# First layer of a two-layer kernel: the spreading of B goes ahead of the sum in TensorE's queue

## The chip, the core and the metric

The kernel runs on one core of one Trainium2 chip. The metric is the device time of one execution in microseconds. Before the change it is 6610.32 us, the median of three runs between 6605.85 and 6630.87 us; the profiled execution spans 6600.6 us.

## What is computed

Two layers follow one another on an input of 4 images of 48 x 48 points with 128 channels. Only the first is touched here. It is a selective scan (a state-space layer) over each image in four directions. Cut to what matters:

```python
xz = einsum(gn(x), in_proj_w); xin, z = split(xz)          # 256 inner channels
xc = silu(depthwise 3x3 convolution of xin)
xs = [xc rows first, xc columns first, and both reversed]    # K = 4 directions, L = 2304 points
dts_r, Bs, Cs = split(einsum(xs, x_proj_w))                 # R = 8, N = 16 states each
dt = softplus(einsum(dts_r, dt_proj_w) + dt_proj_b)
for l in range(L):                                           # for every channel d and state n
    h = h * exp(dt[l] * A) + (dt[l] * xs[l]) * B[l, n]
    y[l] = sum over n of h * C[l, n]
y = y + Ds * xs;  sum of the four directions;  layer norm;  * silu(z);  out_proj;  + x
```

B and C are the same for all channels, and differ by state and by point. The second layer (a Fourier neural operator with attention) starts when the first has ended.

## The kernel before

The channels lie on the partitions, in NF = 2 halves of 128. A direction is cut into chunks of 480 points (the last has 384), and a chunk into N = 16 steps, one for each state. There are 4 x 4 x 5 x 16 = 1280 steps. The work of a step is spread over the engines:

```python
def fetch(u):       # SP: C of two states, broadcast to all partitions by DMA (and B of every fourth state)
def drive_pool(u):  # POOL, for i % 4 == 3 alone: db = du * bbc
    u.db = three.tile([128, NF, LC], F32, tag="db", ...)
    if i % 4 == POOLS: nc.gpsimd.tensor_mul(u.db, c.du, u.bbc)                     # line 329
def spread(u):      # PE, for the other three: B of the state on all 128 partitions, by a matmul
    if i == N - 1: done[0] = c.number + 1
    if i % 4 == POOLS: return
    u.pb = ps_b.tile([128, 512], F32, tag="pb", ...)                                # one buffer
    nc.tensor.matmul(u.pb[:, 0:n], pick[:, i:i+1].to_broadcast([NX, 128]), c.bs[:, 0:n])   # line 339
def drive_in(u):    # DVE, for those three: db = du * pb
    if i % 4 != POOLS: nc.vector.tensor_mul(u.db, c.du, u.pb)                       # line 346
def decay(u):       # ACT: da = exp(dt * A), into PSUM, for each half
    for f in range(NF): nc.scalar.activation(da, c.dt[:, f], AF.Exp, scale=a_neg)   # line 356
def scan(u):        # DVE: h = da * h_before + db along the chunk, for each half
    u.h = three.tile([128, NF, LC], F32, tag="h", ...)                              # three buffers
    for f in range(NF): nc.vector.tensor_tensor_scan(...)                           # line 367
def read_out(u):    # POOL: hc = h * C
    u.hc = three.tile([128, NF, LC], F32, tag="hc", ...)                            # three buffers
    nc.gpsimd.tensor_mul(u.hc, u.h, u.cbc)                                          # line 372
def carry_on(u):    # ACT: the last h, for the next chunk                            # line 375
def sum_up(u):      # PE: adds hc of the 16 states in PSUM, by matmuls with the identity
    if i == 0: ...  # starts the sum with Ds * xc, or with y of the directions before   # lines 384, 389
    for f in range(NF):
        nc.tensor.matmul(c.yp[f], ident, u.hc[:, f], start=False, stop=(i == N - 1))   # line 391
    ...             # after the last state ACT copies yp out                        # lines 399, 406
```

The PSUM pools of the layer are ps_s (2 buffers, for the pieces below), ps_b (1, for pb), ps_a (3, for da) and ps_y (2, for the two halves of yp).

Each call of `advance` starts one step and issues one stage of each of the steps under way. The number is the lag in steps; the order in the tuple is the order of issue, and so the order in each engine's queue. At its end comes one piece of background work: the projections of the next direction's chunks (`project`: px, pd, bs, dt), the front of the next image (`front`: normalization, input projection pj, convolution pc), or the end of a past one (`back`).

```python
LAGS = (
    (0, fetch), (3, drive_pool), (4, drive_in), (5, scan), (4, decay), (5, read_out), (6, carry_on),
    (7, sum_up), (3, spread),
)
def advance(u):
    window.appendleft(u)
    for lag, stage in LAGS:
        if window[lag] is not None:
            stage(window[lag])
    piece()
```

In the middle of each chunk (i = 8) `drive` has POOL compute du = dt * xc of the chunk to come, in two halves (line 245). `project` has POOL compute two small differences for each chunk (lines 227 and 233), which make bs carry B in three bf16 parts.

Of the kernel before, what the change touches and what calls it, by code (L numbers as in the profile page):

```python
# [35 lines left out]
def layer0(ctx, tc, io, x1_dram):  # L36
# [391 lines left out]
    def drain(gen):  # L428
# [3 lines left out]

    LAGS = (
        (0, fetch), (3, drive_pool), (4, drive_in), (5, scan), (4, decay), (5, read_out), (6, carry_on),
        (7, sum_up), (3, spread),
    )
    window = deque([None] * 8, 8)

# [683 lines left out]
```

## Time and profile before

| | before |
|---|---|
| time, median of 3 | 6610.32 us |
| span of the profiled execution | 6600.6 us |
| DVE (VectorE) busy | 5361.8 us, 81% |
| PE (TensorE) busy | 4939.4 us, 75% |
| POOL (GpSimd) busy | 4911.8 us, 74% |
| ACT (ScalarE) busy | 3055.7 us, 46% |
| granted TensorE clock, mean | 0.831 |
| first to last scan of the first layer | 132 to 4494 us |

Busy shares are averages over both layers; the first layer's loop is read by itself from the table of windows. In the list of waits, "A <- B" is idle time of A's engine that ended when B's instruction was done. In the timeline, each row is an instruction or several of one kind in sequence, with its start and its duration, and the idle time before it in brackets. A float32 matmul of the sum appears as two records, so that the two halves of a step make four.

### The profile page before, as it was taken

What the parts mean: (1) busy time and instruction counts of PE and PEld (TensorE: products, weight loads), DVE (VectorE), ACT (ScalarE), POOL (GpSimd) and SP (SyncE); (2) the same over time, 40 slices, a digit from 0 to 9 for tenths busy, and PEclk for the clock granted to TensorE, in tenths of its full rate; (3) what the DMA queues carried; (4) which work ended last, traced back from release to release, by engine and by line L of the source; (5) the groups of instructions that cost most, each with busy time, mean ns of one, the idle gap of its engine ahead of it and who ended that gap; (6) DMA issues with size and microseconds to landing.
All of it is one profiled execution on the core that took longest, in us unless ns stands there. A gap on an engine that the chain in (4) does not pass through costs nothing. (4 is left out here: it accounts for less than half of the span.)

```text
span 6600.6 us, 45820 instructions
## 1 busy us (share of the span) xinstructions
PE 4939.4 (75%) x12490; PEld 2183.8 (33%) x12490; DVE 5361.8 (81%) x5060; ACT 3055.7 (46%) x5657; POOL 4911.8 (74%) x2784
## 2 busy tenths in 40 slices
PE   7898778888887888987887778785323398878763
PEld 3343233334333334333333333332112244435332
DVE  1978889987888998888989888995699899963344
ACT  3656556655656665655666555553000133321222
POOL 2989889888988898898889989883466489951222
PEclk9899989999989999998999998997556655556876
DMA  1222222222223232222323322321300100010222
GB/s 39 89 88 90 93 88 95 88 92 87 91 93 90 89 98 87 92 92 87 96 87 101 91 93 91 93 87 47 68 0 0 16 7 4 4 39 8 58 58 57
DMA packets 271781, 457.67 MB, mean 69 GB/s; under 512 B 87134, under 2 KB 196734, under 8 KB 271522
## 3 DMA queue, kind: packets, MB, share of 16 engines
q1 hardware_dynamic: 224546, 438.13, 22.3%
q10 hardware_dynamic: 46976, 16.61, 1.4%
q8 instruction: 98, 1.61, 0.1%
q14 instruction: 161, 1.32, 0.1%
HBM read 419.60 MB, written 35.02 MB: 69 GB/s over the span
## 5 line engine op out<-in xcount | busy, mean ns | idle before, releaser
L372 POOL TENSOR_TENSOR hc<-h,cbc 128x960 f32<-128x960 f32 (+1 forms) x1280 | 2727.1, 2141 | 495.6 <-DVE h L367 292.5
L391 PE MATMUL yp<-hc,ident 128*128 128x480 f32 (+1 forms) x5120 | 2481.0, 610 | 672.1 <-POOL hc L372 666.7
L356 ACT ACTIVATE da<-dt,a_neg 128x480 f32<-128x480 f32 (+1 forms) x2560 | 1643.7, 647 | 1506.0 <-DVE h L367 1481.2
L367 DVE TENSOR_TENSOR_SCAN h<-da,carry,db 128x480 f32<-128x480 f32 (+1 forms) x2048 | 2304.0, 1175 | 41.6 <-ACT da L356 11.9
L391 PEld LDWEIGHTS yp<-hc,ident 128*128 128x128 f32 x5120 | 992.7, 204 | 2048.7 <-POOL hc L372 1196.8
L346 DVE TENSOR_TENSOR db<-du,pb 128x960 f32<-128x960 f32 (+1 forms) x960 | 1054.3, 1098 | 472.5 <-PE pb L339 423.9
L329 POOL TENSOR_TENSOR db<-du,bbc 128x960 f32<-128x960 f32 (+1 forms) x320 | 685.9, 2143 | 5.0 <-issue 2.5
L887 PE MATMUL py<-attn_t,xt 48*128 48x384 f32 x768 | 507.8, 846 | 78.7 <-DVE m L895 71.9
L367 DVE TENSOR_TENSOR_SCAN h<-da,db 128x384 f32<-128x384 f32 (+1 forms) x512 | 505.6, 1039 | 31.5 <-ACT da L356 24.3
L339 PE MATMUL pb<-bs,pick 112*128 112x480 bf16 (+1 forms) x960 | 368.7, 384 | 66.5 <-DVE db L346 64.0
L889 ACT COPY ysb<-py 128x384 f32<-128x384 f32 x384 | 184.0, 479 | 404.6 <-PE py L887 361.7
L887 PEld LDWEIGHTS py<-attn_t,xt 48*128 48x128 f32 x768 | 233.7, 320 | 339.9 <-issue 148.7
L176 PE MATMUL pc<-pad,cdiag 128*128 128x480 f32 (+1 forms) x720 | 294.0, 549 | 0.3 <-ACT pad L164 0.2
L375 ACT COPY carry<-h 128x2 f32<-128x2 f32 x1280 | 228.5, 179 | 3.7 <-DVE h L367 2.5
L807 PE MATMUL pat<-ident,s 48*48 48x48 f32 x128 | 13.3, 276 | 274.3 <-POOL s L803 274.3
L204 PE MATMUL px<-xc,w_xp 128*112 128x480 f32 (+1 forms) x320 | 212.9, 774 | 2.0 <-ACT xc L188 2.0
L245 POOL TENSOR_TENSOR du<-dt,xc 128x480 f32<-128x480 f32 (+1 forms) x160 | 202.0, 1283 | 7.7 <-DVE db L346 3.3
L900 POOL TENSOR_TENSOR zi<-zi,m 128x384 f32<-128x384 f32 x192 | 192.0, 1000 | 14.5
L898 POOL TENSOR_TENSOR zi<-gw,ysb 128x384 f32<-128x384 f32 x192 | 182.0, 948 | 25.7 <-ACT ysb L889 25.4
L899 POOL TENSOR_TENSOR m<-gw,ysb 128x384 f32<-128x384 f32 x192 | 185.4, 966 | 10.6 <-ACT ysb L889 10.6
L389 PE MATMUL yp<-y,ident 128*128 128x480 f32 (+1 forms) x240 | 170.6, 832 | 18.6 <-ACT y L406 18.3
L339 PEld LDWEIGHTS <-pick 112*128 112x128 bf16 x960 | 101.1, 105 | 251.5 <-issue 229.4
(263 smaller groups left out, 5808.2 us busy)
## 6 DMA issues: line engine op xcount, KB each, us to landing
cbc<-cd SPq DMA_DIRECT2D x512, 480.0 KB
bbc<-cd SPq DMA_DIRECT2D x256, 240.0 KB
cbc<-cd SPq DMA_DIRECT2D x128, 384.0 KB
bbc<-cd SPq DMA_DIRECT2D x64, 192.0 KB
da_wM<-a_wM SPq DMA_DIRECT2D x12, 396.0 KB
x<-in_xT SPq DMA_DIRECT2D x16, 288.0 KB
xr<-in_xT SPq DMA_DIRECT2D x16, 288.0 KB
e_wM<-de_wM SPq DMA_DIRECT2D x12, 384.0 KB
```

The source lines that it names most:

```text
L176: nc.tensor.matmul(pc[:, 0:n].rearrange("p (r c) -> p r c", c=H), cdiag[:, j], pad[:, r0 + dy : r0 + dy + nr, dx : dx + H], start=(j == 0) ...
L204: nc.tensor.matmul(like(px[0:NX, 0:n], k), w_xp[:, k, f], src[:, f], start=(f == 0), stop=(f == NF - 1))
L245: nc.gpsimd.tensor_mul(like(c.du[:, f, 0:n], c.k), like(c.dt[:, f, 0:n], c.k), src[:, f])
L329: nc.gpsimd.tensor_mul(u.db[:, :, 0:n], c.du[:, :, 0:n], u.bbc[:, :, 0:n].to_broadcast([128, NF, n]))
L339: nc.tensor.matmul(u.pb[:, 0:n], pick[:, i : i + 1].to_broadcast([NX, 128]), c.bs[:, 0:n], start=True, stop=True)
L346: nc.vector.tensor_mul(u.db[:, :, 0:n], c.du[:, :, 0:n], u.pb[:, None, 0:n].to_broadcast([128, NF, n]))
L356: nc.scalar.activation(da[:, 0:n], c.dt[:, f, 0:n], AF.Exp, scale=a_neg[:, q, i : i + 1])
L367: nc.vector.tensor_tensor_scan(ha, aa, ba, init, ALU.mult, ALU.add)
L372: nc.gpsimd.tensor_mul(u.hc[:, :, 0:n], u.h[:, :, 0:n], u.cbc.to_broadcast([128, NF, n]))
L375: nc.scalar.copy(carry[:, u.i], u.h[:, :, 0 if u.c.k >= 2 else u.c.n - 1])
L391: nc.tensor.matmul(c.yp[f][:, 0:n], ident, u.hc[:, f, 0:n], start=False, stop=(i == N - 1))
L887: nc.tensor.matmul(p[:, 0 : HG * T], xt[:, c, j], attn_t[:, b, hs], start=True, stop=True)
```

## The change

In the tuple that orders the stages, `spread` of step t-3 is moved ahead of `sum_up` of step t-7. Both are TensorE's alone, but for the copies of yp by ACT at the end of a chunk, so TensorE's queue has the two in the other order. Its purpose is that the spreading of B for a coming state need not stand in the queue behind a sum that waits for its product.

```diff
     LAGS = (
         (0, fetch), (3, drive_pool), (4, drive_in), (5, scan), (4, decay), (5, read_out), (6, carry_on),
-        (7, sum_up), (3, spread),
+        (3, spread), (7, sum_up),
     )
```

## The prediction

> **What bounds the kernel now.** I first read the page's row of slices, to see which part of the span the change can touch. Each digit is a tenth of busy time in a fortieth (165 us) of the span.
>
> ```profile
> PE   7898778888887888987887778785323398878763
> DVE  1978889987888998888989888995699899963344
> POOL 2989889888988898898889989883466489951222
> ```
>
> The first layer's scan loop fills slices 1 to 27: the scans of line 367 run from 132 to 4494 us, 4363 us of the 6601 us span. In it DVE and POOL are both at eight or nine tenths, and neither is full. The table of windows over this stretch gives DVE 3856 us busy, POOL 3830, PE 3586 and ACT 2583. So the loop is a pair of almost equal servers, each idle for about 500 of 4363 us, that take turns in waiting for one another. The second layer, after 4500 us, holds none of the changed lines.
>
> Next I asked who waits for whom in the stretch. Columns: the engine and line that waited, the engine and line that released it, total us, times, longest.
>
> ```profile
> ACT da L356 <- DVE h L367: 1481.2, 1713, 7.1
> PE yp L391 <- POOL hc L372: 666.4, 436, 5.8
> DVE db L346 <- PE pb L339: 423.9, 270, 7.8
> POOL hc L372 <- DVE h L367: 292.5, 268, 4.3
> POOL hc L372 <- PE yp L391: 144.1, 89, 4.8
> PE pb L339 <- DVE db L346: 64.0, 75, 2.2
> DVE h L367 <- ACT da L356: 36.2, 24, 6.4
> ```
>
> ACT's wait is the longest and of no account: ACT has 1780 us to spare. DVE's idle time is the third row, 424 us, nearly all it has: it waits for pb, B spread over the partitions, a matmul of 0.38 us. PE isn't full either, so why is so short a matmul late? The second row tells: PE itself stands before the sum (line 391) waiting for POOL's product hc. The timeline shows the coupling at one spot (start us, duration, engine, line, and the idle time before with its releaser). DVE's own part:
>
> ```profile
> 2999.93 2.32 DVE L367 TENSOR_TENSOR_SCAN h<-da,carry,db 128x480 f32<-128x480 f32 x2
> 3006.01 1.15 DVE L346 TENSOR_TENSOR db<-du,pb 128x960 f32<-128x960 f32 x1 [3.77 <-PE pb L339]
> 3007.09 2.32 DVE L367 TENSOR_TENSOR_SCAN h<-da,carry,db 128x480 f32<-128x480 f32 x2
> ```
>
> POOL's, at the same time:
>
> ```profile
> 2998.57 1.44 POOL L245 TENSOR_TENSOR du<-dt,xc 128x480 f32<-128x480 f32 x1
> 2999.96 2.21 POOL L372 TENSOR_TENSOR hc<-h,cbc 128x960 f32<-128x960 f32 x1
> 3002.25 1.09 POOL L233 TENSOR_TENSOR bs<-xd,bs 16x480 bf16<-16x480 f32 x1
> ```
>
> And PE's:
>
> ```profile
> 3002.23 3.55 PE L391 MATMUL yp<-hc,ident 128*128 128x480 f32 x4 [4.17 <-POOL hc L372]
> 3005.59 0.39 PE L339 MATMUL pb<-bs,pick 112*128 112x480 bf16 x1
> ```
>
> POOL was busy with du for the next chunk, so hc came at 3002.17. PE had stood idle for 4.17 us before the sum that needs it, and the spreading, whose inputs (bs of the chunk, a free pb since 3000.01) had long been there, was next in the queue. DVE lost 3.77 us to a product it has no use for.
>
> [...] the spreading at 3005.59 starts only when the sum ends, though its inputs are ready. [...] Here the four sum records after 4.17 us of idleness took 3.55 us, and the same four 1.77 us elsewhere, so a long stall costs DVE another 1.8 us. [...]
>
> **The change, part by part.** No instruction is added or taken away: 960 spreadings and 1280 sums stay, and PE's busy time stays. Within one call of the loop's body PE's order was sum(t-7), spread(t-3), background piece; it becomes spread(t-3), sum(t-7), piece. What changes is the lap of waits that ties POOL's delay to DVE.
>
> Before, hc of step r holds up sum(r), and so spread(r+4). The lap until hc of step r+4: sum 1.8, spread to DVE 0.4, drive_in(r+4) 1.1, scan(r+3) 2.2, drive_in(r+5) 1.1, scan(r+4) 2.2, hc product 2.2, together 11.0 us for four steps (durations from the timeline; a pair of scans adds 2.23). DVE alone needs 3 x 1.05 + 4 x 2.23 = 12.1 us for four steps. So only **1.1 us** of POOL delay fits in before DVE stops. But POOL owes extra work in lumps: two du products of 1.34 us and two corrections of bs of 1.09 us for every chunk, 4.9 us, and every fourth step a product db of 2.22.
>
> After, hc(r) holds up sum(r), then the piece, then spread(r+5). The lap is 11.0 us plus the piece for five steps, in which DVE alone needs 4 x 1.05 + 5 x 2.23 = 15.3. Pieces on PE are 0, 1.07 (pd), 1.77 (px) or, where the next image's convolution runs, 2.58 us. The slack becomes 4.3 us less the piece, on the average some **3 us** against 1. Put otherwise, every wait of DVE that POOL causes through PE gets shorter by up to some 2 to 3 us.
>
> How much of the 424 us is of that kind? Walking through the 270 waits in the timeline and looking at PE before each, about 268 us had PE waiting for hc first; another 55 us had PE only in late sums, catching up. In the remaining 100 or so PE was full of other work: some 55 us of it beside the convolution (line 176), where four steps cost PE four sums of 1.45, three spreadings of 0.37 and three pieces of 2.58, 14.7 us against DVE's 12.1, the rest at chunk borders with the four strided matmuls of line 389 (3.4 us) and in the last parts of an image. There two successive spreadings have one sum and one piece between them in either order, and pb is single, so I expect nothing.
>
> Sizes: some 140 of the waits are under 1 us, 59 under 2, 28 under 3, 23 under 4, 21 under 5, three over 6. Cutting 3 us from each leaves about 12 + 29 + 14 = 55 us of the whole 424, so some 230 of the 268 us can fall, and half of the 55 us, 27: together about **257 us**. Some comes back. POOL is as loaded as DVE: a DVE that no longer stops for pb will at times stop at the ring of three h buffers, scan(t-5) needing the hc product of t-8. POOL's floor is 3830 busy, 43 at the start and 144 waiting for free hc buffers, 4017 against 4363, so 346 us is the cap, and one fifth to a quarter given back seems right. That leaves about **200 us**: 6610 - 200 = 6410.
>
> **The rivals.** First: **the wait only moves to h.** The row DVE h <- POOL hc has 6.7 us in all now, and that could be because pb always stops DVE first. If POOL sets the pace anyway, DVE stops there for most of the 424 us and the time stays at 6560 to 6610. Against it: POOL itself idles 292 us for h, which means that it isn't the pacemaker all of the time; DVE's stops make it idle later, as one of 0.88 us before 3013 shows, some 7 us after DVE's stop above.
>
> Second: **the sum is now held up by DVE.** Spread(t-3) waits until drive_in(t-4) has read pb, and the sum stands behind it. That row, PE pb <- DVE db, is 64 us now and will grow. Sums free the hc buffers, and POOL <- PE yp is 144 us already. If both grew by 100 us, POOL would lose what DVE wins and the kernel would be the same or slower, 6600 to 6680. Against it: hc product(u) needs scan(u), which ends some 5.5 us after drive_in(u), and the sum it needs, u-3, is freed by that same drive_in(u), and takes 0.4 + 1.8 us; it has 3.3 us to spare, less only than a long piece.
>
> Third: **the gain is fuller**, since a PE that idles less stays at full clock, and stalls lead to further stalls: 300 us or more, 6300.
>
> **Range and chances.** 6410 is the middle; 6290 is near the cap, 6560 has the first rival for the most part. Two per cent is 132 us, and my expected gain is 200 with some 100 either way: faster by over 2% 0.70, within 2% 0.25, slower 0.05.
>
> **What the profile after would show.** DVE db <- PE pb falls from 424 to about 150, and of that mostly beside the convolution and at chunk borders. DVE h <- POOL hc rises from 7 to some tens of us, PE pb <- DVE db from 64 to 100 or more, POOL hc <- DVE h falls by 100 or more, POOL hc <- PE yp stays within 50 of 144. The loop ends about 4300 us instead of 4497, and the second layer keeps its length. I am wrong if the convolution stretches, not the lumps on POOL, hold most of the loss, or if DVE h <- POOL hc takes over hundreds of us.

## The result, and the profile after

The changed kernel takes 6541.4 us (median of 4 runs, 6529.45 to 6547.69) against 6608.23 us (median of 4): a ratio of **0.9889, interval 0.9863 to 0.9915**, a gain of 1.1% or 67 us. The time lies inside the stated range of 6290 to 6560. The size of the gain did not come out: 200 us were expected.

The three rows of slices of the page after, as they were shown of before:

```profile
PE   7798878889877889887888777785233398878763
...
DVE  1988889988989998888999898994699999963444
...
POOL 2989889888999898888989999882565489951222
```

The loop's last scan starts at 4418 us, not at 4492; the second layer is as long as before. DVE and POOL still show eights and nines. Who waits for whom in the loop (columns as in the prediction):

```profile
ACT da L356 <- DVE h L367: 1364.1, 1663, 6.8
...
PE yp L391 <- POOL hc L372: 566.5, 423, 4.6
DVE db L346 <- PE pb L339: 353.8, 209, 5.9
...
POOL hc L372 <- DVE h L367: 237.1, 216, 4.7
PE pb L339 <- DVE db L346: 139.0, 154, 3.3
...
POOL hc L372 <- PE yp L391: 107.7, 66, 3.8
...
DVE h L367 <- ACT da L356: 43.4, 17, 6.0
...
DVE h L367 <- POOL hc L372: 11.7, 14, 1.1
```

DVE's wait for pb fell by 70 us only, from 424 to 354, and with it the time. No other wait of DVE or POOL took its place: their rows for h, for hc, for yp and for da are small or smaller. PE's own wait for drive_in grew, from 64 to 139. So neither of the first two rivals happened. The wait that was to go is simply still there. The timeline of after shows how. POOL's row first, at the place in a chunk where it computes du:

```profile
2952.78 1.09 POOL L227 TENSOR_TENSOR xd<-xd,bs 48x480 f32<-48x480 f32 x1
2953.95 2.83 POOL L245 TENSOR_TENSOR du<-dt,xc 128x480 f32<-128x480 f32 x2
2956.73 2.23 POOL L372 TENSOR_TENSOR hc<-h,cbc 128x960 f32<-128x960 f32 x1
```

Then PE's and DVE's:

```profile
2952.75 3.32 PE L391 MATMUL yp<-hc,ident 128*128 128x480 f32 x4 [2.50 <-POOL hc L372]
2955.87 0.61 PE L339 MATMUL pb<-bs,pick 112*128 112x480 bf16 x1
2959.01 2.76 PE L391 MATMUL yp<-hc,ident 128*128 128x480 f32 x4 [2.54 <-POOL hc L372]
2961.56 0.61 PE L339 MATMUL pb<-bs,pick 112*128 112x480 bf16 x1
...
2962.20 1.16 DVE L346 TENSOR_TENSOR db<-du,pb 128x960 f32<-128x960 f32 x1 [2.30 <-PE pb L339]
```

This is the picture of before: hc is late at 2958.96, PE stands idle for 2.54 us ahead of the sum, which then takes 2.76 us in place of 1.77, and the spreading comes out behind it at 2961.56. DVE has lost 2.30 us. The source has the spreading ahead of the sum.

The listing of the program as built tells what happened. The order of the stages in the source is not yet the order of the queue: when the program is built, a scheduler arranges each engine's instructions anew. I counted, for each of the 960 spreadings, how many sums stand before it in PE's queue; the records of the traces, in order of time, give the same counts. A lead of 3 means right behind sum(x-4), of 4 right ahead of it, of 3.5 between the two halves of that sum.

```
lead in steps            5    4   3.5    3   2.5    2   (start)
before, as built         3   41     2  732   147   33      2
changed, as built        0  434   203  234    83    4      2
as the source asks       0  957     0    0     0    0      3
```

**Less than half of the spreadings had moved.** The trace of before held a sign of it that I didn't read. There a spreading stands between two rows of two sum records each, which the source never asks for:

```profile
3029.91 1.07 PE L391 MATMUL yp<-hc,ident 128*128 128x480 f32 x2 [0.41 <-POOL hc L372]
3030.82 0.37 PE L339 MATMUL pb<-bs,pick 112*128 112x480 bf16 x1
3031.02 0.97 PE L391 MATMUL yp<-hc,ident 128*128 128x480 f32 x2
```

DVE's order moved too, though no line of it was changed: drive_in stands a whole step ahead of its own scan 331 times before and 476 times after, right before it 242 and 181 times.

### The profile page after: what moved, and what is told of

Its sections match the earlier page's. It is cut to its first block, busy times and chain, and to the rows that moved or that the text cites. A ratio compares the mean times of both kernels' runs of the same rounds, so it can differ in the third digit from the quotient of the medians.

```text
span 6527.3 us, 45804 instructions
## 1 busy us (share of the span) xinstructions
PE 4892.4 (75%) x12490; PEld 2172.5 (33%) x12490; DVE 5348.1 (82%) x5060; ACT 3047.5 (47%) x5657; POOL 4906.7 (75%) x2784
## 5 line engine op out<-in xcount | busy, mean ns | idle before, releaser
L391 PE MATMUL yp<-hc,ident 128*128 128x480 f32 (+1 forms) x5120 | 2438.7, 599 | 570.8 <-POOL hc L372 566.5
```

Source lines behind the costliest of these rows:

```text
L391: nc.tensor.matmul(c.yp[f][:, 0:n], ident, u.hc[:, f, 0:n], start=False, stop=(i == N - 1))
```

## The experiments

Theory A: the lap of waits in the prediction is right, and half of the change was never carried out. Theory B: POOL and ACT set the pace with their lumps whatever PE's order is. Theories C and D: DVE's order, which changed unasked, is what counts. By C it matters more than PE's; by D its shift took back about 100 us.

**1. Carry the order out.** The helper pins an instruction behind the one issued before it on the same engine, in issue order alone, with no wait added:

```diff
+    pin = tc.keep_in_program_order
-        nc.tensor.matmul(u.pb[:, 0:n], pick[...], c.bs[:, 0:n], ...)
+        pin(nc.tensor.matmul(u.pb[:, 0:n], pick[...], c.bs[:, 0:n], ...))
-            nc.tensor.matmul(c.yp[f][:, 0:n], ident, u.hc[:, f, 0:n], ...)
+            pin(nc.tensor.matmul(c.yp[f][:, 0:n], ident, u.hc[:, f, 0:n], ...))
```

On the changed kernel, a_pe: 

> The changed kernel, with each spreading and each sum pinned behind the instruction before it in TensorE's queue, so that all 956 spreadings of the steady loop stand four steps ahead of the sums (in the changed kernel as built only 434 of them do, 203 stand between the halves of a sum, and 317 stand behind the sum as before). Theory A, the lap argument holds and half of the change was never carried out by the scheduling at build time: the time falls by another 70 to 130 us, to 6410 to 6470, and DVE db <- PE pb falls from 354 to under 250. Theory B, lumps of work on POOL and ACT set the pace whatever the order in PE's queue: 6510 to 6560, and the wait for pb stays over 300 or turns into waits for da or h.

Measured: 6387.2 us, ratio 0.9667 (0.9652 to 0.9682), 154 us below the changed kernel. That is far from theory B's range, and more than theory A foresaw: its direction has a first support, its size was too small.

On the kernel before, b_pe: 

> The kernel before with the same pins, so that 946 spreadings stand three steps ahead, right behind the sum (732 of them do as built, 147 stand half a step lower, 41 a step higher). Both theories: within 25 us of before, 6585 to 6635. It shows what the pins alone do.

Measured: 6652.1 us, ratio 1.0066 (1.0049 to 1.0084). A little slower than foreseen: the first scan starts at 158 us in place of 132.7, since spreadings are pinned behind the first direction's pieces. So pins as such gain nothing, and with the same pins on both sides the swap is worth 265 us (6652 to 6387).

With `pin` around drive_in and the scans as well, a_pedve: 

> As a_pe, and on DVE drive_in and scan pinned too, so that drive_in of a step always stands a whole step ahead of its scan (as built in the changed kernel: 476 a step, 284 half a step, 181 right before their own scan). Theory A with the lap as worked out: same as a_pe within 20 us or up to 40 better, as pb comes free earlier. Theory C, that the place of drive_in in DVE's queue matters more than that of the spreading in PE's: over 40 us better than a_pe. Theory B: as a_pe, 6510 to 6560.

Measured: 6596.2 us, ratio 0.9989 (0.9982 to 0.9996). A miss for every theory: 209 us worse than a_pe.

And b_pedve: 

> The kernel before with pins on PE and DVE: spreadings three steps ahead, drive_in a whole step ahead of its scan. This is the kernel that my lap of 11.0 us describes. Theory A: slower than before by 0 to 60 us, since drive_in that comes before the older scan lengthens that scan's wait: 6610 to 6670. Theory C: faster than before by over 40 us. The difference between b_pedve and a_pedve is the whole worth of the change when both orders are carried out as written: 150 to 200 us by theory A, under 60 by theory B.

Measured: 6981.1 us, ratio 1.0573 (1.0553 to 1.0593). Far out of the range. The order of change is worth 385 us here, but a drive_in that comes a whole step early can stop DVE ahead of a scan that was ready (in the trace before, 192 of the 270 waits for pb, 299 of the 424 us, had such a scan of an older step behind them), and these pins also tie DVE to its other work, so the pair doesn't show which of the two costs more.

**2. DVE's part, and two ways to go further.** a_pe_dasafter gives DVE the order of the changed kernel, by pins at the listed places: 

> a_pe with DVE's order pinned to that of the changed kernel as built (drive_in a whole step ahead of its scan 495 times, between the halves 284, right before it 181), so that against the changed kernel only TensorE's order differs. If the order in TensorE's queue alone is behind the 154 us between the changed kernel and a_pe: within 25 us of a_pe, 6365 to 6410. If the shift in DVE's order that came with the pins (368, 342, 237) had a good part in it: 6425 to 6480.

Measured: 6493.1 us, ratio 0.9836 (0.9821 to 0.9852), outside both ranges. It could be DVE's order or the pins to DVE's other work; the third group separates them.

a_pe_d2 issues drive_in after the scan of the step before (the edit in effect, shortened):

```diff
-        (0, fetch), (3, drive_pool), (4, drive_in), (5, scan), ...
+        (0, fetch), (3, drive_pool), (5, scan), (4, drive_in), ...   # both pinned, as in a_pe
```

> a_pe with drive_in always right before its own scan on DVE, and so behind the scan of the step before. By the lap of waits, a late pb then holds up no older scan: the lap is sum 1.8, spread 0.4, drive_in 1.1, scan 2.2, product 2.2 us and the piece, 7.7 us for five steps in place of 11.0, so less waiting for pb and 6300 to 6370. The rival: the spreading of the next step and the sum behind it now wait for a later drive_in, the hc buffers come free too late, POOL hc <- PE yp rises over 150 us, and the time is 6400 to 6500.

Measured: 6484.3 us, ratio 0.983 (0.9815 to 0.9846). The rival's number: POOL waits 159.3 us for yp, and PE waits 583.2 us for drive_in, twice that of a_pe. This kernel too has DVE tied to its other work, so not all of its loss need be the later drive_in.

a_chain links spreadings and sums to one another and leaves the pieces free:

```diff
+    last_ = [None]
+    def pin(r):                      # issue order behind the spreading or sum before it
+        if last_[0] is not None: tc.add_manual_dep(r.ins, last_[0].name, <NoSync>, reason="chain")
+        last_[0] = r.ins; return r
```

> As a_pe, but spreadings and sums are pinned to one another alone and not to the pieces, which stay free. The same lead of four steps. The first scan started 29 us later in a_pe (161.5 us) than in the changed kernel (132.9), since the spreadings stood behind the pieces of the first direction. Expected: that start comes back, and the rest stays: 6350 to 6375. If the pins against the pieces did part of the work: over 6390.

Measured: 6363.1 us, ratio 0.9645 (0.9629 to 0.9661). As expected; the late start was the pins'.

a_lag8 takes the sum a step later still:

```diff
-        (3, spread), (7, sum_up),
+        (3, spread), (8, sum_up),           # pinned as in a_pe; the window is 9 long
-        u.hc = three.tile(...)
+        u.hc = four.tile(...)
```

> a_pe with the sum one step later still (lag 8) and four buffers for hc, so that the spreading stands five steps ahead of the sums. By the lap theory one more step of slack: DVE db <- PE pb falls further, and DVE waits for h or da in its place: 6310 to 6380. If what is left in a_pe is the work of POOL and the convolution pieces on PE, which no order changes: 6375 to 6400.

Measured: 6328.6 us, ratio **0.9594 (0.9577 to 0.9611)**, the fastest of those that compute the whole result. PE's wait for hc is down to 32.5 us. This one still has the late start. It also has a fourth hc buffer, which was not run by itself, so how much of the 59 us below a_pe is the longer lead isn't shown.

**3. PE's and DVE's orders apart.** Here the source is left as it is, and after the loop a chain of issue order is laid through spreadings and sums, and another through drive_ins and scans, in any order I give by code. Nothing else is tied.

```diff
+    def tie(short, long, code):     # code: how many of `long` stand before each of `short`
+        ...
+        for p_, q_ in zip(line, line[1:]): tc.add_manual_dep(q_.ins, p_.ins.name, <NoSync>)
+    tie(spreadings, sum_halves, <PE's order>);  tie(drive_ins, scan_halves, <DVE's order>)
```

t_ab: 

> The changed kernel with the order of spreadings and sums on TensorE tied to just what it is in the changed kernel as built (lead four steps 434 times, three and a half 203, three 234, less 87), and the order of drive_in and scans on DVE tied to what it is in the kernel before (drive_in a whole step ahead of its scan 331 times, half 370, none 242; as built in the changed kernel 476, 284, 181). Theory D, the change moved DVE's order too, and that took back about 100 us: 6420 to 6470. Theory A alone, DVE's order weighs little and the 106 us lost in a_pe_dasafter came from pinning DVE to its other work: 6520 to 6550.

t_ba: 

> The kernel before with TensorE's order tied to its own and DVE's order tied to that of the changed kernel as built. Theory D: slower by about as much as t_ab is faster, 6670 to 6730. Theory A alone: 6590 to 6625.

t_4a: 

> All spreadings four steps ahead on TensorE, as in a_chain, and DVE's order tied to that of the changed kernel as built; nothing is tied to other work. Theory D: 6450 to 6490, as in a_pe_dasafter less its late start. Theory A alone: 6355 to 6400.

t_4b: 

> All spreadings four steps ahead on TensorE and DVE's order tied to that of the kernel before: the change as it stands in the source, carried out for all steps, and nothing else. Both theories, as a_chain: 6345 to 6400. Its distance from before is the worth of the order that the prediction reckoned with (about 200 us by it), and its distance from the changed kernel is what the building lost.

Measured, with the two kernels in their places (us, ratio to before with its interval):

| PE's order | DVE's order of before | DVE's order of the changed kernel |
|---|---|---|
| of before | 6606 (before) | t_ba 6739.4, 1.0202 (1.0184 to 1.022) |
| of the changed kernel | t_ab 6541.9, 0.9902 (0.9888 to 0.9917) | 6541.4 (changed), 0.9889 |
| lead 4 everywhere | t_4b 6368.2, 0.964 (0.9626 to 0.9655) | t_4a 6398.9, 0.9686 (0.9669 to 0.9703) |

Theory D falls: with PE's order of the changed kernel, DVE's order makes no difference (6542 and 6541). It does matter beside the other two orders of PE: 133 us in t_ba, which lies outside the ranges of both theories, and 31 in t_4a. Of the 94 us between a_pe_dasafter and t_4a about 30 are the late start (the first scan at 162.3 us and at 132.3). The other 64 or so came from ties to other work, and mostly DVE's, since a_pe and a_chain differ by 24 us in all. PE's order alone, carried out, brings 238 us; as built, 64.

POOL's order moved unasked as well, and no run ties it. Between two products hc, POOL has over 3.5 us of other work 51 times in the trace of before, 45 times in the changed kernel's and 21 times in t_4b's. That alone isn't the gain: b_pe, with 17 such places, takes 6652 us.

The waits of t_4b:

```profile
PE pb L339 <- DVE db L346: 330.8, 354, 2.4
PE yp L391 <- POOL hc L372: 280.2, 217, 4.0
...
DVE db L346 <- PE pb L339: 155.0, 118, 3.8
...
POOL hc L372 <- DVE h L367: 115.5, 114, 4.3
POOL hc L372 <- PE yp L391: 87.4, 59, 4.5
...
DVE h L367 <- POOL hc L372: 34.5, 50, 1.3
```

And a place of the same kind in its timeline, one chunk earlier than the rows of the changed kernel above, where POOL's xd, one half of du and bs stand in a row from 2806.80 to 2810.58. PE, then DVE:

```profile
2809.42 0.36 PE L339 MATMUL pb<-bs,pick 112*128 112x480 bf16 x1 [0.77 <-DVE db L346]
2812.93 3.31 PE L391 MATMUL yp<-hc,ident 128*128 128x480 f32 x4 [3.15 <-POOL hc L372]
...
2811.43 1.13 DVE L346 TENSOR_TENSOR db<-du,pb 128x960 f32<-128x960 f32 x1
2812.91 2.33 DVE L367 TENSOR_TENSOR_SCAN h<-da,carry,db 128x480 f32<-128x480 f32 x2 [0.36 <-POOL hc L372]
2816.49 1.22 DVE L367 TENSOR_TENSOR_SCAN h<-da,carry,db 128x480 f32<-128x480 f32 x1 [1.25 <-POOL hc L372]
```

PE still waits 3.15 us for hc, but the spreading is already out, at 2809.42, held by drive_in alone. drive_in follows at 2811.43 without a wait, and DVE stops for 0.36 and 1.25 us at the ring of three h buffers, which is where the prediction saw the next limit. In the very chunk of the rows above it comes out less well (PE, then DVE):

```profile
2863.84 3.02 PE L391 MATMUL yp<-hc,ident 128*128 128x480 f32 x4 [2.71 <-POOL hc L372]
2866.66 1.79 PE L204 MATMUL px<-xc,w_xp 128*112 128x480 f32 x2
2868.28 0.38 PE L339 MATMUL pb<-bs,pick 112*128 112x480 bf16 x1
...
2868.70 1.15 DVE L346 TENSOR_TENSOR db<-du,pb 128x960 f32<-128x960 f32 x1 [2.45 <-PE pb L339]
```

Here a late sum and then a px stand ahead of the spreading of the next step, and DVE still loses 2.45 us. Waits of this kind make up some 50 of the 155 us that are left.

**4. The dose, the lumps and the places.** Ties as in t_4b, other orders. t_35b: 

> DVE's order as in the kernel before, and on TensorE every spreading between the two halves of the sum (lead three and a half steps, 957 times). Lap theory: the spreading still waits for the same hc product as before, and only half a sum (0.9 us) is taken out of the lap, so a third of the way at most: 6520 to 6570. If the mean lead counts: half way from before to t_4b, 6470 to 6505.

Measured: 6587.0 us, ratio 0.9969 (0.9958 to 0.998). A miss by 17 us: the half step brought less than the lap allowed.

t_3b: 

> DVE's order as in the kernel before, and on TensorE every spreading right behind the sum (lead three steps, 957 times; as built 732, with 180 lower and 44 higher). Lap theory and mean lead: 6570 to 6625. If it is the few places with less lead that cost most: 6520 to 6560, as those 180 are mended.

Measured: 6759.5 us, ratio 1.023 (1.0215 to 1.0245). A miss: slower than before by 153 us. In its list of waits POOL stands 225.6 us for yp, before's 144, and DVE 553.4 for pb. With one and the same order on DVE, leads of 3, 3.5 and 4 steps take 6759, 6587 and 6368 us: 172 us for the first half step, 219 for the second. The next run shows that most of the first lies in one place of the chunk.

t_3b_edge mends one place of t_3b: 

> t_3b with the 80 spreadings of state 4 raised to a lead of four steps, so that they stand ahead of the chunk's first sum, which waits for the copies of yp and has four more matmuls (as built in the kernel before, 41 of the 80 are there). If t_3b is 153 us slower than before because of this place: 6570 to 6640. If it is the mismatch of the two orders elsewhere: over 6690.

Measured: 6596.0 us, ratio 0.9982 (0.9973 to 0.999). That place is all of it, and POOL's wait for yp is down to 120.7 us: the 80 spreadings at a chunk's border, of which the kernel before had 41 ahead of the first sum as built, are worth 163 us with DVE's order held. They cost less where DVE's order is free: in b_pe's trace all 80 stand behind the first sum too, but drive_in of state 4 stands right before its own scan 79 times, against 35 in t_3b, and the time is 6652, 107 us below t_3b in spite of the late start. That it is this place of DVE's order which helps is read from the two traces, not shown by a run. Against t_3b_edge (6596), the lead of three and a half steps (6587) gains 9 us only, though with its own border spreadings half a step lower; so away from the border no larger gain of a half step is shown.

du left out but for the first chunk, so that all chunks use the first one's, on the kernel before and on t_4b:

```diff
     def drive(c):
+        if kept: c.du = kept[0]; return
         ...
+        kept.append(c.du)
```

t_bb_nodu: 

> The kernel before, TensorE and DVE tied to its own order, with du computed for the first chunk alone and used for all (158 products of 1.28 us, 203 us of POOL, left out; the output isn't the reference's). If POOL's lumps cause the stops at pb: DVE db <- PE pb falls by over 120 us and the time to 6430 to 6500. If the lumps are hidden: over 6560.

t_4b_nodu: 

> t_4b with du left out in the same way. If the lead of four steps already hides the lumps: down by less than 80 us, 6290 to 6345. If POOL's total work sets the pace: down by as much as the kernel before (t_bb_nodu), 6180 to 6270.

Measured: 6460.2 us, ratio 0.9779 (0.9763 to 0.9795), and 6279.8 us, ratio 0.9508 (0.9489 to 0.9528). The kernel before, tied to its own orders, falls by 146 us, t_4b by 88, between its two ranges. The row of t_bb_nodu against 424 of before:

```profile
DVE db L351 <- PE pb L344: 297.5, 259, 7.8
```

The du lumps are thus behind a good part of the wait, 126 us by this row; the longer lead hides some of them, not all. Both runs also take some 200 us of work off POOL in all, so lump and load are not told apart.

t_ab_12, last, raises two places of each chunk: 

> t_ab (TensorE as in the changed kernel as built, DVE as before) with the spreadings of states 1 and 2 of each chunk alone raised to a lead of four steps: 129 of the 523 that are below it. These two stand behind the sums of states 13 and 14 of the chunk before, whose products come late because POOL's du lump stands right before hc of state 13; as built only 29 of 160 have the full lead. If the build lost the gain there, where the lump falls: at least half of the 174 us between t_ab and t_4b comes back, 6368 to 6455. If every place counts alike: a quarter, 43 us, 6485 to 6515.

Measured: 6453.2 us, ratio 0.9763 (0.9738 to 0.9788). 129 places, a quarter of those below the full lead, bring 89 us, half of what t_ab lacks against t_4b. The build had given the full lead to most spreadings of states 4, 5 and 8, and to 29 of 160 right behind POOL's lump, where it is needed.

## Why the prediction was wrong, point by point

- **The step that failed** is the one written as "Within one call of the loop's body PE's order was sum(t-7), spread(t-3), background piece; it becomes spread(t-3), sum(t-7), piece." I took the order of the source for the order of the queue. In the queue as built 434 of 958 spreadings stood there, and few of them behind POOL's lumps. All the rest of the sum then applied to a part only: the 257 us gross and 200 net came out as 67. That 6541 lies inside the range is luck: its upper end was meant for a wait that moves to h, and that didn't happen.
- With the order carried out the sum holds: 238 us gained in t_4b, against 200; 269 us off DVE's wait for pb, against 257 gross; DVE's wait for pb 155.0 us, against "about 150"; DVE's wait for h 34.5 ("some tens"); PE's wait for drive_in 330.8 ("100 or more"); POOL's wait for h down by 177 ("by 100 or more"). POOL's wait for yp fell by 57, a little more than "within 50". The loop's last scan starts at 4256 us ("about 4300").
- **What was to stay did.** Of the 155 us left in t_4b, some 58 have convolution records (line 176) on PE during the wait, counted in its trace; the prediction put some 55 there. (Its sum for that place, 14.7 us against 12.1, sets sums of a chunk of 384 points, 1.45 us, beside DVE's time for 480; the 55 us came from the waits themselves.) Another 50 or so lie behind a late hc with px as the piece in between, which the lap allowed for ("The slack becomes 4.3 us less the piece").
- **The lap's size.** Its slack of 1.1 us described a queue that wasn't there either: b_pedve, in which drive_in stands a whole step ahead as I reckoned, takes 6981 us. In the kernel before, 242 drive_ins stand right before their own scan. The direction and rough size of one step of lead came out; that they did with a slack reckoned for another queue is luck in part.
- **The chunk's border** was left out by "so I expect nothing". t_3b and t_3b_edge differ by 163 us in just that place, with DVE's order held. A likely reason, which no run shows, is that a spreading ahead of the chunk's first sum also escapes the wait for the copies of yp (at lines 384 and 389 PE stands 46.3 us for them in t_3b, 34.3 in t_3b_edge). As built 41 of 80 stood there before and 78 of 80 after, so a part of the change's own 67 us may come from this place; no run shows how much.
- **The rivals.** The wait did not move to h (11.7 us), and the sum was held up by DVE for 75 us more with no harm: POOL's wait for yp fell. Both stay out in t_4b.

What stays open: why the mixed order of before (6606) is as good as a uniform lead of 3 with the border mended (6596), though 180 of its places have less lead, how much of the loss of a_pedve is early drive_ins and how much the ties to other work, and what the shift in POOL's order is worth.

## What to carry to other kernels

Where a program is arranged by a scheduler at build time, a swap in the source is only a wish: list the queue as built and count before reckoning with the new order, and look in the old trace for sequences that the source doesn't have. When an order matters, tie it, but tie only the instructions concerned to one another: ties to everything on the engine cost some 64 us on DVE, by the difference above, and some 25 us at the start on PE. And a lead is needed most where the lumps fall: there a quarter of the places without it gave half of the gain that was missing.

## What the runs showed of the hardware beyond that

PE's granted clock was low after waits shorter than the 4.17 us of the prediction's rows, too. In the changed kernel's trace four sum records take 1.77 us with a granted clock of 1.00 (at 2966.38). After 2.50 us of idleness, at 2952.75 in the rows shown, they took 3.32 with a granted clock of 0.54. Of the sums of 480 points that waited for hc in this trace, 8 of 138 took over 2.3 us after a wait under 1.5 us, 21 of 42 after 2 to 3 us, and all 23 after more than 3 us. So in this trace a long wait for hc is paid twice, by the wait and by a slow sum, and a short one seldom is. The means of whole runs go the same way: with PE's wait for hc at 667 us before, 567 in the changed kernel, 280 in t_4b and 33 in a_lag8, a record of the sum takes 610, 599, 584 and 577 ns in the mean.
